# Half-norm statistics two and two behind the masks of the next two steps, and the second transposition of x1 behind the first half's feed-forward products

## The chip, the cores and the metric

The kernel runs on one core of one Trainium2 chip. The metric is the device time of one execution in microseconds. The matrix engine is called PE (its weight loads PEld), the vector engine DVE, the scalar engine ACT, GpSimd POOL, and SP issues most of the DMAs. Each engine works through its own instruction queue in order, and waits on semaphores for the others.

## What is computed

Sixteen graphs (`x`: 16 x 1024 x 128, one adjacency matrix 1024 x 1024 for all) go through three transformer-like layers and a last graph-attention layer. In short, for each batch element and layer:

```python
Q, K, V = h @ Wq, h @ Wk, h @ Wv                  # 8 heads of 16
scores = einsum('bnhd,bmhd->bhnm', Q, K) / sqrt(16)
scores = where(adj == 0, -inf, scores)
attn_out = einsum('bhnm,bmhd->bnhd', softmax(scores), V)
x = layer_norm(h + attn_out @ Wo + bo)            # norm 1, with gain and bias
y = relu(x @ W1 + b1) @ W2 + b2                   # 128 -> 256 -> 128
x = layer_norm(x + y)                             # norm 2
```

The last layer computes `h = x @ W`, an attention weight exp(leaky_relu(s_i + s_j)) over the neighbours, the weighted sum, adds x and normalises again. Everything is in float32.

## The kernel before, in words

**Blocks and steps.** The work is cut into 48 blocks, one for each batch element and layer (four batch elements go through the three layers in turn, so that blocks 0-3 are layer 0 of elements 0-3, blocks 4-7 layer 1, and so on). A block has 32 steps: 2 head groups x 2 halves of the queries x 8 key tiles (`kt`). A step (`score_step`) computes the scores of four heads as two PSUM tiles of 128 x 1024, by four matmuls (L423, "s"). Of these two tiles the second always gets its mask added by DVE (L433) and its exponential from ACT (L445); the first goes the same way where kt is 1, 5 or 7, and else gets its exponential first (ACT L430) and is multiplied by a 0/1 mask on POOL (L431). So a step has one or two DVE masks. There are three such PSUM slots ("s"), so the scores of a step have to wait until the masks or exponentials of the step before last and of the last one have read theirs. Four steps later (`AHEAD`) the exponentials are multiplied with V into one PSUM bank ("acc", L450). When a half of the queries has had its eight steps, `finish` reads this one bank with a DVE transposition (L461, "tt"), and the next accumulation has to wait for that.

In this document a step of a block is called step 0 to 31; M9 stands for the DVE mask of step 9 (M9a and M9b where there are two), E9 for the exponential after it, X10 for the exponential read straight from PSUM, P10 for the POOL mask.

**The other work is cut into pieces,** functions that are taken one a step by `piece()` behind the step's scores and products: the projections of the next block (`proj_tasks`: two transpositions, Wk, Wq and V by halves; `split` copies a half of K or Q out of PSUM as a rounded part "hi" by ACT, L385, and then the rest "lo" by DVE, L386), what follows the attention (`post_tasks`), and the last layer's pieces (`last_tasks`: nodes, edges, aggregates) for every batch element that has left its third layer. `post_tasks` has, for each half h of the nodes: `out_proj(h)` (32 small PE products with Wo), `x1t(h)` (four PE transpositions and an ACT copy; the second one also issues the two POOL operations of `scale_shift`), `ffn1(0, h)` and `ffn1(1, h)` (8 products and an ACT relu each) and `ffn2(h)` (64 small products). All of these go through one PSUM bank ("t"), so that a piece waits until the result of the piece before has been read.

**The steps at which pieces become due** are written in the table AT (L34). Before, the pieces behind the attention stood at steps 12 (out_proj 0), 22 (out_proj 1), 23 and 25 (x1t 0 and 1), 26, 27, 28 and 30 (ffn1), and 32 and 40 (ffn2, that is steps 0 and 8 of the block after). The projections are due at steps 3, 6, 9, 11, 14, 17, 19 and 20. The last layer's pieces have gaps instead of steps. A piece that is due has to wait where another chain's piece is taken in the same step.

**A half norm.** `out_proj` and `ffn2` end with `add_and_stats`: DVE adds the product to x (L329, with a raised priority), then come four `bn_stats` (L322) and four `bn_aggr` (L324), one for each of the half's four node tiles; then `normalise` issues seven operations on POOL (L337 to L341).

**Who sets the order.** PE and ACT run in the order in which the program issues (`manual_schedule`). DVE and POOL are ordered by the framework's scheduler by priorities, and their order is then fixed in the program too. `tc.issue_after(x)` makes instructions stand behind x; `behind["dve"]` is the last mask that DVE was given.

The two quoted lines are those that matter most below, the order of the pieces and the rule for a half norm:

```python
together = [(5, both, "+w +w"), (1, out_proj(0), "-w"), (1, out_proj(1), "-w"), (5, x1t(0), "+w"), (1, x1t(1), "+w")]
project([s["aT", h]], [w["Wo"]], h, add_and_stats(s["n1"]))
```

Of the kernel before, what the change touches and what calls it, by code (L numbers as in the profile page):

```python
# [30 lines left out]
FIRST = 1  # L31


AT = {"proj": (3, 6, 9, 11, 14, 17, 19, 20), "post": (12, 22, 23, 25, 26, 27, 28, 30, 32, 40, 41)}  # L34
AT_END = {3: (12, 21, 22, 24, 25, 26, 27, 28, 30, 31), 2: (8, 9, 13, 14, 15, 16, 17, 18, 20, 21)}
AHEAD = 4
BOTH_ON_DVE = (1, 5, 7)
# [78 lines left out]
def fast_path(ctx: ExitStack, tc: tile.TileContext, a: dict, out: bass.AP, flag):  # L116
    nc = tc.nc
# [201 lines left out]
    def stats(n, ts):  # L319
        z, st, mv = n  # L320
        for t in range(ts.start, ts.stop):
            nc.vector.bn_stats(st[:, t, :], z[:, t, :])  # L322
        for t in range(ts.start, ts.stop):
            nc.vector.bn_aggr(mv[:, t, :], st[:, t, :])  # L324

    def add_and_stats(n):
        def out(ts, ps):
            with soon():
                nc.vector.tensor_add(n[0][:, ts, :], v3(ps), n[0][:, ts, :])  # L329
            stats(n, ts)  # L330
        return out

    def normalise(n, ts):

# [64 lines left out]
    behind = {}  # L399
# [66 lines left out]
        return run  # L466


    def post_tasks(b, l):
        w = W[l]  # L470
        s = {}
        att, recs = state["A"], state["recs"]

        def gather(h):
            def run():
                s["aT", h] = half_tile("aT")
                nc.vector.transpose(s["aT", h], att[:, h].rearrange("p k g d -> p (k g d)"))
                if h == 1:
                    check_range(recs.rearrange("p g h k -> p (g h k)"))
            return run  # L480

        def out_proj(h):
            def run():
                if h == 0:
                    s["n1"] = with_stats(state["x", b])
                project([s["aT", h]], [w["Wo"]], h, add_and_stats(s["n1"]))
                normalise(s["n1"], slice(4 * h, 4 * h + 4))
            return run

        def x1t(h, alone=False):  # L490
            def run():
                x1 = s["n1"][0]
                s["x1T", h] = transpose_half("x1T", x1, h, w["ln1_gc"], w["ln1_bc"])
                if alone:
                    scale_shift(x1[:, 4 * h:4 * h + 4, :], w["ln1_g"], w["b2"])
                elif h == 1:
                    scale_shift(x1, w["ln1_g"], w["b2"])
            return run

        def ffn1(f, h):  # L500
            def run():
                s["h", f, h] = half_tile("hT")
                ps = bank()
                by_columns(ps, w["W1"][:, f * P:(f + 1) * P], s["x1T", h])
                with soon():
                    nc.scalar.activation(s["h", f, h], ps, AF.Relu, bias=w["b1"][:, f:f + 1], scale=1.0)
            return run

        def ffn2(h):
            def run():  # L510
                if h == 0:
                    s["n2"] = with_stats(state["x", b])
                project([s["h", f, h] for f in range(NF)], [w["W2"][:, f, :] for f in range(NF)], h,
                        add_and_stats(s["n2"]))
                normalise(s["n2"], slice(4 * h, 4 * h + 4))
            return run

        def both():
            gather(0)()
            gather(1)()  # L520


        together = [(5, both, "+w +w"), (1, out_proj(0), "-w"), (1, out_proj(1), "-w"), (5, x1t(0), "+w"), (1, x1t(1), "+w")]
        for h in range(2):
            together += [(1, ffn1(0, h), "+w"), (1, ffn1(1, h), "+w -w")]
        together += [(1, ffn2(0), "-w -w"), (1, ffn2(1), "-w -w")]
# [129 lines left out]
    chains = []  # L656
# [15 lines left out]
    def take(chain):  # L672

        _, f, tiles, mark, _ = chain["queue"][0]
        if any(free[t[1:]] == 0 for t in tiles.split() if t[0] == "+"):
            return False
        chain["queue"].popleft()
        f()
        for t in tiles.split():
            free[t[1:]] += -1 if t[0] == "+" else 1  # L680
        done.add(mark)
        chain["due"] = now[0]
        if not chain["queue"]:
            chains.remove(chain)
        return True

    def is_due(chain):
        gap, at = chain["queue"][0][0], chain["queue"][0][4]
        return now[0] >= (chain["due"] + gap if at is None else at)

    def piece():
        for chain in chains:
            if is_due(chain) and take(chain):
                return

    def need(mark):
        while mark not in done:
# [29 lines left out]
    def av_due(n):  # L727

        for item in [w for w in waiting if w[2] <= n]:
            step, e, _ = item  # L730
            half = step[:3]
            if half not in accs:
                if accs:
                    continue
                accs[half] = sums
                left[half] = NT
            waiting.remove(item)
            left[half] -= 1
            av_step(step, e, accs[half], left[half] == NT - 1, left[half] == 0)
            if left[half]:  # L740
                continue
            m, g, qh = half
            b, l = blocks[m]
            while g == 0 and qh == 0 and last_attn:
                need(last_attn.pop())
            finish(g, qh, accs.pop(half))()
            if m == len(blocks) - 1:
                if g == G - 1:
                    if qh == 0:
                        final.append(post_tasks(b, l)[1])  # L750
                    put(final[0][qh], ("final", qh), first=True)
                    if qh == 1:
                        put(last_tasks(b), ("last", b), chains[0])
            elif g == G - 1 and qh == 1:
                post = post_tasks(b, l)[0]
                chain = put(post[:1], ("attn", b, l))
                put(post[1:], ("post", b, l), chain, table=AT_END.get(len(blocks) - m))
                last_attn.append(("attn", b, l))
                if l == L - 1:
                    put(last_tasks(b), ("last", b), chain)  # L760
# [291 lines left out]
```

## Time and profile before

| what | value |
|---|---|
| median of 3 runs | 3961.19 us (3955.6 to 3964.78) |
| time of the profiled execution | 3958.22 us, span 3956.1 us, mean granted clock 0.988 |
| busy in the span | PE 95%, DVE 86%, ACT 85%, POOL 84% |
| masks on DVE (L433) | 2112, mean 1214 ns |
| `bn_stats` (L322), `bn_aggr` (L324) | 896 each, mean 278 and 154 ns |
| x add (L329), "tt" (L461), "lo" (L386) | mean 691, 706 and 680 ns |
| one block without last-layer pieces | 72.5 us |

The page gives for each engine its busy time, and by groups of instructions how long one takes and what ended the idle time before it. A view by windows gives the same for stretches of the span, with the clock that PE was granted (1.00 is full). The span falls into regular parts: blocks 2-9, 15-21, 27-33 and 39-45 take 72.5 us each; in blocks 11-14, 23-26 and 35-38 the last layer's pieces of four batch elements run as well, and they take 92.5 to 100.8 us; blocks 10, 22 and 34, where those begin, take 76.6 us. The rest is the start, blocks 46 and 47, and the end behind the last step.

### The profile page before, as it was taken

Reading aid. Unit: us, or ns where it says so; the run is one execution under the profiler, and the core shown is the slowest. Engines: PE = TensorE matmul, PEld = TensorE weight load, DVE = VectorE, ACT = ScalarE, POOL = GpSimd, SP = SyncE. Lnnn points to the kernel's source line nnn. Section 1 sums busy time; section 2 is a strip of 40 time slices with the busy share of each in tenths; the row PEclk is TensorE's granted clock in tenths of the full one; section 3 lists DMA queues with packets and bytes.
Section 4 is the critical chain, followed back from the end, with each engine's and each line's share of the span. In section 5 each row is a group of like instructions: output and inputs, shape, how many; then the busy total and the mean of one; then the engine's idle time right before and its main releaser. Section 6 shows DMA issues by size and latency. Waiting matters only on the chain.

```text
span 3956.1 us, 107747 instructions
## 1 busy us (share of the span) xinstructions
PE 3770.4 (95%) x44501; PEld 1552.3 (39%) x44501; DVE 3407.3 (86%) x5326; ACT 3371.7 (85%) x3961; POOL 3329.4 (84%) x3010
## 2 busy tenths in 40 slices
PE   7999999999999999999999999999999999999996
PEld 2333333344443333334444333333444433333345
DVE  7898998988888998988888898998888898898874
ACT  7999999977779999997777999999777799999860
POOL 5788988978789888988778898889877898898875
PEclk8999999999999999999999999999999999999998
DMA  6222222112222222222222222221222222222200
GB/s 164 65 65 57 53 65 65 49 43 65 55 58 61 65 65 54 55 65 56 55 56 56 65 54 56 65 65 47 56 55 56 68 50 59 65 56 54 66 8 20
DMA packets 124465, 233.13 MB, mean 59 GB/s; under 512 B 34624, under 2 KB 73792, under 8 KB 123968
## 3 DMA queue, kind: packets, MB, share of 16 engines
q1 hardware_dynamic: 123056, 225.74, 22.7%
q8 instruction: 354, 5.80, 0.6%
q14 instruction: 143, 1.17, 0.1%
q10 hardware_dynamic: 912, 0.42, 0.0%
HBM read 15.54 MB, written 8.39 MB: 6 GB/s over the span
## 4 chain that ended last, share of the span: by engine, by line
PE 66%; DVE 26%; POOL 3%; issue 3%; ACT 1%; SPq 0%; DMA 0%; DVEq 0%; POOLq 0%; ACTq 0%
PE acc L450 24%; PE t L297 20%; PE s L423 18%; DVE e L433 16%; DVE st L322 3%; PE t L286 2%; DVE tt L461 1%; DVE lo L386 1%; DVE mv L324 1%; POOL e L431 1%; PE s L297 1%; PE s L607 1%; DVE x L329 1%; POOL x L345 1%; DVE e L610 1%
## 5 line engine op out<-in xcount | busy, mean ns | idle before, releaser
L433 DVE TENSOR_TENSOR e<-s,mask_add 128x1024 f32<-128x1024 f32 x2112 | 2492.7, 1214 | 323.7 <-PE s L423 309.3
L445 ACT ACTIVATE e<-e 128x1024 f32<-128x1024 f32 x2112 | 2189.6, 1062 | 281.5 <-DVE e L433 266.7
L431 POOL TENSOR_TENSOR e<-e,mask 128x1024 f32<-128x1024 f32 x960 | 1934.3, 2028 | 300.5 <-ACT e L430 300.1
L450 PE MATMUL acc<-e,v 128*17 128x512 f32 x12288 | 1625.9, 601 | 32.1 <-DVE tt L461 23.0
L423 PE MATMUL s<-Wq,Wk 64*128 64x512 f32 x6144 | 1198.1, 458 | 62.1 <-DVE e L433 29.2
L430 ACT ACTIVATE e<-s 128x1024 f32<-128x1024 f32 x960 | 982.4, 1023 | 168.9 <-PE s L423 168.8
L423 PEld LDWEIGHTS s<-Wq,Wk 64*128 64x128 f32 x6144 | 500.1, 185 | 1046.0 <-issue 439.1
L450 PEld LDWEIGHTS acc<-e,v 128*17 128x17 f32 x12288 | 207.4, 95 | 538.1 <-issue 466.2
L341 POOL TENSOR_SCALAR x<-x,mv 128x128 f32<-128x128 f32 x896 | 389.7, 449 | 23.5
L337 POOL TENSOR_SCALAR mv<-mv 128x4 f32<-128x4 f32 x224 | 53.0, 237 | 236.2 <-DVE mv L324 188.6
L339 POOL TENSOR_TENSOR mv<-mv,half_neg 128x4 f32<-128x4 f32 x224 | 232.4, 1038 | 18.6
L345 POOL TENSOR_TENSOR x<-x,ln_g 128x1024 f32<-128x1024 f32 (+1 forms) x97 | 230.1, 2372 | 9.5 <-PE t L286 7.1
L297 PE MATMUL t<-hd,e 128*32 128x129 f32 x7040 | 208.3, 275 | 0.0
L329 DVE TENSOR_TENSOR x<-t,x 128x512 f32<-128x512 f32 x191 | 132.0, 691 | 83.5 <-PE t L297 77.1
L297 PEld LDWEIGHTS t<-hd,e 128*32 128x32 f32 x7040 | 194.7, 110 | 14.1 <-issue 4.7
L297 PE MATMUL t<-x1T,W 128*32 128x512 f32 x1520 | 198.2, 593 | 0.0
L322 DVE BATCH_NORM_STATS2 st<-x 128x6 f32<-128x128 f32 x896 | 196.4, 278 | 0.7
L297 PEld LDWEIGHTS t<-W,hT 128*32 128x32 f32 x6080 | 169.9, 110 | 58.5 <-issue 35.3
L297 PE MATMUL t<-W,hT 128*32 128x128 f32 x6080 | 183.4, 273 | 0.2 <-DVE x L625 0.2
L286 PEld LDWEIGHTS t<-identf,x 128*128 128x128 f32 x872 | 92.9, 141 | 230.3 <-issue 118.2
L286 PE MATMUL t<-identf,x 128*128 128x128 f32 x872 | 150.5, 288 | 33.5 <-DVE lo L386 19.6
L610 DVE SCALAR_TENSOR_TENSOR e<-s,mask 128x1024 f32<-128x1024 f32 x128 | 150.3, 1213 | 6.4 <-PE s L607 5.0
(118 smaller groups left out, 2569.5 us busy)
## 6 DMA issues: line engine op xcount, KB each, us to landing
Wk<-hi SPq DMA_DIRECT2D x384, 128.0 KB
Wk<-lo SPq DMA_DIRECT2D x384, 128.0 KB
Wq<-hi SPq DMA_DIRECT2D x384, 128.0 KB
Wq<-lo SPq DMA_DIRECT2D x384, 128.0 KB
x<-in_x_dram SPq DMA_DIRECT2D x16, 512.0 KB
out_dram<-x SPq DMA_DIRECT2D x31, 256.0 KB
ai<-in_adj_dram SPq DMA_DIRECT2D x8, 512.0 KB
g_rows<-parts SPq DMA_DIRECT2D x124, 4.0 KB
```

What stands on the lines that cost most here:

```text
L286: nc.tensor.transpose(ps[:, t * P:(t + 1) * P], src[:, 4 * h + t, :], identf)
L297: nc.tensor.matmul(dst[j:j + SLOT, :], lhsT[:, j:j + SLOT], rhs, start=start, stop=stop)
L322: nc.vector.bn_stats(st[:, t, :], z[:, t, :])
L339: nc.gpsimd.tensor_tensor(v, v, half_neg[:, ts], OP.pow)
L341: nc.gpsimd.tensor_scalar(z[:, t, :], z[:, t, :], mv[:, t, 0:1], mv[:, t, 1:2], op0=OP.add, op1=OP.mult)
L345: nc.gpsimd.tensor_mul(z, z, rows(gain, n))
L423: nc.tensor.matmul(ps[:, r * 512:(r + 1) * 512], k[64 * r:64 * r + 64, kt * P:(kt + 1) * P], q[64 * r:64 * r + 64, q0:q0 + 512], start=Tru ...
L430: nc.scalar.activation(ev, psv, AF.Exp, scale=HD ** -0.5)
L431: behind["pool"] = nc.gpsimd.tensor_mul(ev, ev, m).ins
L433: behind["dve"] = nc.vector.tensor_add(ev, psv, m).ins
L445: nc.scalar.activation(ev, ev, AF.Exp, scale=HD ** -0.5)
L450: nc.tensor.matmul(acc[j * SLOT:j * SLOT + HD + 1, :], v_bufs[m % 2][:, kt, 2 * j + g, :], e[:, j, :], start=first, stop=last)
```

## The change

In all blocks but those whose follow-up work belongs to the end (there `quick` stays true, and all is as before):

- The four `bn_stats` and four `bn_aggr` of a half norm are no longer issued right behind the x add. They become two pieces of their own: `first` has two `bn_stats`, `rest` the other two, the four `bn_aggr` and then `normalise`. Each is to stand behind the last DVE mask that was issued by then. Such a piece has a star and does not use up its step: another piece may be taken in the same step.
- The second transposition of x1 (`x1t(1)`) moves from step 25 to step 28, and the first half's two feed-forward products from 26 and 27 to 25 and 26; those of the second half from 28 and 30 to 30 and 31.
- `x1t(0)` has a gap of 1 where it had 5; its step in the table stays 23.

```diff
-AT = {"proj": (3, 6, 9, 11, 14, 17, 19, 20), "post": (12, 22, 23, 25, 26, 27, 28, 30, 32, 40, 41)}
+AT = {"proj": (3, 6, 9, 11, 14, 17, 19, 20), "post": (12, 13, 14, 22, 23, 23, 24, 25, 26, 28, 30, 31, 32, 33, 34, 40, 41, 42)}
...
-    def add_and_stats(n):
+    def add_and_stats(n, now=True):
         def out(ts, ps):
             with soon():
                 nc.vector.tensor_add(n[0][:, ts, :], v3(ps), n[0][:, ts, :])
-            stats(n, ts)
+            if now:
+                stats(n, ts)
         return out
+
+    def norm_later(n, h):
+
+        def first():
+            z, st, _ = n()
+            with tc.issue_after(behind["dve"]):
+                for t in range(4 * h, 4 * h + 2):
+                    nc.vector.bn_stats(st[:, t, :], z[:, t, :])
+
+        def rest():
+            z, st, mv = n()
+            with tc.issue_after(behind["dve"]):
+                for t in range(4 * h + 2, 4 * h + 4):
+                    nc.vector.bn_stats(st[:, t, :], z[:, t, :])
+                for t in range(4 * h, 4 * h + 4):
+                    nc.vector.bn_aggr(mv[:, t, :], st[:, t, :])
+            normalise(n(), slice(4 * h, 4 * h + 4))
+        return [(1, first, "*"), (1, rest, "*")]
...
-                project([s["aT", h]], [w["Wo"]], h, add_and_stats(s["n1"]))
-                normalise(s["n1"], slice(4 * h, 4 * h + 4))
+                project([s["aT", h]], [w["Wo"]], h, add_and_stats(s["n1"], quick))
+                if quick:
+                    normalise(s["n1"], slice(4 * h, 4 * h + 4))
...
-                        add_and_stats(s["n2"]))
-                normalise(s["n2"], slice(4 * h, 4 * h + 4))
+                        add_and_stats(s["n2"], quick))
+                if quick:
+                    normalise(s["n2"], slice(4 * h, 4 * h + 4))
...
+            together += [(1, out_proj(0), "-w")] + norm_later(n1, 0) + [(1, out_proj(1), "-w")] + norm_later(n1, 1)[:1]
+            together += [(1, x1t(0), "+w")] + norm_later(n1, 1)[1:]
+            together += [(1, ffn1(0, 0), "+w"), (1, ffn1(1, 0), "+w -w"), (1, x1t(1), "+w")]
+            together += [(1, ffn1(0, 1), "+w"), (1, ffn1(1, 1), "+w -w")]
+            together += [(1, ffn2(0), "-w -w")] + norm_later(n2, 0) + [(1, ffn2(1), "-w -w")] + norm_later(n2, 1)
...
     def piece():
-        for chain in chains:
-            if is_due(chain) and take(chain):
-                return
+        for chain in list(chains):
+            while chain["queue"] and is_due(chain):
+                alone = "*" not in chain["queue"][0][2]
+                if not take(chain):
+                    break
+                if alone:
+                    return
...
-                post = post_tasks(b, l)[0]
+                post = post_tasks(b, l, len(blocks) - m in AT_END)[0]
```

The number of instructions on each engine is the same in both programs; their order is not. Of DVE's order the program as built shows this for a block without last-layer pieces (steps 0 to 16; `st`, `mv`: statistics; `chk`, `recs`: small):

```
before: M0 x M1a st*4 mv*4 M1b M2 M3 tt M4 .. M8 aT*2 x M9a st*4 mv*4 M9b lo M10 M11 tt recs lo M12 x M13a st*4 mv*4 M13b M14 M15a lo M15b M16
after:  M0 x M1a M1b st*2 M2 st*2 mv*4 M3 tt M4 .. M8 aT*2 x M9a M9b lo M10 st*4 mv*4 M11 tt lo recs M12 x M13a M13b st*2 M14 M15a lo M15b st*2 mv*4 M16
```

More of the change, by code (lines that the diff above doesn't have):

```diff
@@ L466, in finish, with post_tasks @@
         return run
-    def post_tasks(b, l):
+    def post_tasks(b, l, quick=True):
         w = W[l]
@@ L520, in both, with n1, n2 @@
             gather(1)()
[L523 to L526, printed above, removed]
+        def n1():
+            return s["n1"]
+        def n2():
+            return s["n2"]
+        together = [(5, both, "+w +w")]
+        if quick:
+            together += [(1, out_proj(0), "-w"), (1, out_proj(1), "-w"), (5, x1t(0), "+w"), (1, x1t(1), "+w")]
+            for h in range(2):
+                together += [(1, ffn1(0, h), "+w"), (1, ffn1(1, h), "+w -w")]
+            together += [(1, ffn2(0), "-w -w"), (1, ffn2(1), "-w -w")]
+        else:
+            together += [(1, out_proj(0), "-w")] + norm_later(n1, 0) + [(1, out_proj(1), "-w")] + norm_later(n1, 1)[:1]
[3 more added lines that the diff above has]
+            together += [(1, ffn2(0), "-w -w")] + norm_later(n2, 0) + [(1, ffn2(1), "-w -w")] + norm_later(n2, 1)
         alone = [[(1, gather(h), "+w"), (1, out_proj(h), "-w"), (3, x1t(h, True), "+w"), (1, ffn1(0, h), "+w"),
@@ L678, in take @@
         f()
-        for t in tiles.split():
+        for t in tiles.replace("*", "").split():
             free[t[1:]] += -1 if t[0] == "+" else 1
```

## The prediction, made before the changed kernel was run

> **What bounds the kernel now.** I read the page first (busy shares), then the windows block by block, then the waits of one plain block, then its timeline. The page's first line shows four engines that are all busy:
>
> ```profile
> PE 3770.4 (95%) x44501; PEld 1552.3 (39%) x44501; DVE 3407.3 (86%) x5326; ACT 3371.7 (85%) x3961; POOL 3329.4 (84%) x3010
> ```
>
> The windows (start:end, length, then busy time of PE, PEld, DVE, ACT, POOL; clock; DMA) show one plain block (5) and blocks 11 to 14:
>
> ```profile
> 389.20:461.70 72.50, 71.11 (x726) 25.80 (x722) 65.19 (x97) 68.85 (x79) 64.59 (x57) 1.00 0.24 59
> ...
> 828.20:924.20 96.00, 91.51 (x1333) 44.30 (x1329) 82.30 (x141) 71.85 (x91) 76.46 (x75) 0.98 0.23 57
> 924.20:1021.30 97.10, 90.30 (x1334) 44.16 (x1331) 81.11 (x140) 72.10 (x91) 77.16 (x75) 1.00 0.22 56
> 1021.30:1122.10 100.80, 93.85 (x1341) 44.97 (x1337) 81.30 (x140) 73.04 (x92) 78.63 (x76) 0.97 0.21 55
> 1122.10:1214.70 92.60, 89.84 (x1286) 42.32 (x1282) 78.69 (x134) 69.92 (x81) 76.58 (x76) 1.00 0.23 59
> ```
>
> In a plain block PE is idle for 1.4 us of 72.5, ACT for 3.6, DVE for 7.3. The waits in that block (engine, line, releaser: total, times, longest) say how little of this is the matter of half norms:
>
> ```profile
> DVE e L433 <- PE s L423: 6.2, 10, 1.2
> ...
> ACT e L445 <- DVE e L433: 3.3, 5, 1.1
> ...
> PE s L423 <- ACT e L430: 0.5, 1, 0.5
> PE s L423 <- DVE e L433: 0.5, 2, 0.2
> PE acc L450 <- DVE tt L461: 0.4, 2, 0.2
> ```
>
> So DVE's idle time lies where PE has long pieces and DVE waits for scores; elsewhere DVE runs without a break. The DVE timeline (start, duration) of steps 9 to 12, then ACT's "hi" and PE's next accumulation:
>
> ```profile
> 410.02 0.69 DVE L329 TENSOR_TENSOR x<-t,x 128x512 f32<-128x512 f32 x1
> 410.63 1.21 DVE L433 TENSOR_TENSOR e<-s,mask_add 128x1024 f32<-128x1024 f32 x1
> 411.76 0.86 DVE L322 BATCH_NORM_STATS2 st<-x 128x6 f32<-128x128 f32 x4
> 412.54 0.36 DVE L324 BATCH_NORM_AGGREGATE mv<-st 128x2 f32<-128x6 f32 x4
> 412.82 1.19 DVE L433 TENSOR_TENSOR e<-s,mask_add 128x1024 f32<-128x1024 f32 x1
> 413.93 0.68 DVE L386 TENSOR_TENSOR lo<-t,hi 128x512 fp32r<-128x512 f32 x1
> 414.53 2.35 DVE L433 TENSOR_TENSOR e<-s,mask_add 128x1024 f32<-128x1024 f32 x2
> 416.79 0.70 DVE L461 STREAM_TRANSPOSE tt<-acc 128x512 f32<-128x512 f32 x1
> ```
> ```profile
> 412.90 0.57 ACT L385 CAST hi<-t 128x512 fp32r<-128x512 f32 x1
> ```
> ```profile
> 417.64 1.05 PE L450 MATMUL acc<-e,v 128*17 128x512 f32 x8 [0.18 <-DVE tt L461]
> ```
>
> To see: a mask takes 1.13 us of DVE (start to start), a half norm's eight statistics 1.06 (411.76 to 412.82), "lo" 0.60. "tt" comes after all of it, and PE's accumulation starts 0.85 behind "tt" (416.79 to 417.64). From step 1 to 19 it is DVE's sum of work, not the place of the statistics in it, that sets PE.
>
> **The change, in a plain block (29 of them).** Counts stay; 16 `bn_stats` and 16 `bn_aggr` a block (four bursts of 1.06 us) move. I laid the new order of DVE, ACT and PE on the rows of this block, with these intervals, and looked where PE leaves the old times. No DMA moves; SP's order is as before.
>
> *Steps 1 to 8 (norm 2, first half).* x add at 392.75 as before, since PE's ffn2 sets it. M1b comes 1.06 earlier, but the statistics still stand before "tt" of step 3, which starts at about 398.95 (before: 398.91). PE gains 0.24 in step 3 and loses it in front of the accumulation of step 4. ACT is 0.2 to 0.3 earlier, a slot of step 7 with it: -0.17. Bounds: 0 and -0.73 (what step 2 took above its 1.64).
>
> *Steps 9 to 12 (norm 2, second half).* Here the change adds a wait. "lo" stood behind M9b, and the statistics filled the time until "hi" was done (412.90 + 0.57 = 413.47). Now M9b starts at 411.67 and DVE is through with its issue at 412.80 (times 0.16 earlier by the step above); "hi" can't move, because on ACT it stands behind E9a, and E9a behind M9a. It ends at 413.32, so DVE stands for 0.56 in front of "lo". Behind it are M10, the four statistics, M11 and "tt", which starts at 417.28 in place of 416.79; PE's only accumulation bank waits for it: +0.49 at step 13, measured against before. Bounds: 0 if "hi" were ready, 0.6.
>
> *Steps 13 to 19 (norm 1, first half).* The second two statistics and the aggregates come behind M15b (the projection at 14 takes that step), in front of M16 and M17a. M17a is 0.78 late, of which 0.49 are inherited. E17a waits for it, "hi" of step 17 and X18 stand behind E17a on ACT, and the second slot of step 19 waits for X18: PE +0.72 at step 20, so this step adds 0.23. Bounds: 0 and 0.5.
>
> *Steps 23 to 25 (norm 1, second half).* The burst leaves M23b, which held step 25's first slot. But its second slot is set by x add, M23a, E23a, the copy of x1T and X24 in a row, which nothing moves: 0.
>
> *Steps 25 to 31.* x1t(1) at step 25 waited for its norm (the step took 2.74, and 2.23 without a wait as in step 6). At 28 it doesn't. The four ffn1 pieces take 2.50 wherever they stand. Steps 23 to 31 come to 0.27 less. One ffn1 relu falls behind E31, where ACT idles for 1.14 in step 2 anyway; the two POOL operations of `scale_shift` (2.4 each) go from behind P24 to behind P28, and ffn2's x add needs them only after step 32, some 3 us later: no cost; were POOL later by more than that, this add and M1a behind it would wait.
>
> Sum: 0.72 - 0.27 = +0.45 a block, 29 blocks: **+13 us**; bounds -0.1 and +0.8 a block.
>
> **Blocks 10 to 14 and their like (three groups).** Here pieces slip to other steps.
> - Block 11: the first edges come at step 1. DVE had the burst between M1a and M1b, then two edges, and PE stood:
>
> ```profile
> 835.81 0.50 PE L423 MATMUL s<-Wq,Wk 64*128 64x512 f32 x2 [1.66 <-DVE e L433]
> ```
> ```profile
> 836.00:840.00 4.00, 3.37 (x20) 0.97 (x22) 3.26 (x4) 2.53 (x3) 3.89 (x6) 0.77 0.73 169
> 840.00:844.00 4.00, 4.00 (x28) 1.11 (x22) 3.36 (x5) 3.21 (x5) 3.05 (x4) 0.81 0.02 6
> ```
>
>  After that wait the clock is 0.77 and 0.81 (0.23 x 4 + 0.19 x 4 = 1.7 us lost). Now the burst stands behind the edges and M2; the wait falls to about 0.6, and step 4 starts up to 2.6 earlier; taken as -1.9, since the clock may dip all the same. Waits for "lo" in steps 15 and 16 go (-1.1), others come in steps 25 to 31 (+0.6): -2.4.
> - Blocks 12 to 14: the first edges move from step 4 to 7, in front of a long piece (-1.0, -2.3, -1.5 for the three), and pieces leave crowded steps (15, 23 to 25, 29: together -3.7 in 12 and 13). Against it: "lo" of step 9 now stands behind M10 and an edge, and the aggregate of step 10 needs its bank: +1.3 in each. And the last aggregate slips from 16 to 21, so that POOL has between P22 and P24 a norm (3.5), `scale_shift` (4.9) and the end's pair (2.7): 11 us. P24 ends 16.6 us behind the start of step 22, the accumulation that needs it could start at 13.3: +3.3 in 12 and 13, and, by the row above, another clock dip (+1.7); x1t(1) follows `rest` by two steps there (+0.75; +0.5 in 14). In all about +2.4, +1.1 and 0.
> - Block 10: 0. A clock dip that only the first group has in block 13 (0.97 against 1.00) may go: -2.
>
> Group: -2.4 + 2.4 + 1.1 = +1, three of them +3, less 2: **+1 us**; bounds -15 and +25, as both waits on POOL and clock come or not. What else moves is named and costs nothing while POOL has its 8 us of idle time a plain block.
>
> [...]
>
> **Total:** +14. The profiled execution took 3958.2 (span 3956.1 and 2.1 around it), 0.07% under the median 3961.19; the share is the same, so 3961 + 14 = **3975 us**.
>
> **Rivals.**
> 1. *Faster, about 3932.* PE's gaps behind masks and exponentials (0.5 + 0.5 a block) were what the bursts cost; they vanish, 29 x 1.0. For it: the first x add's burst is followed by a gap of 0.52. Against it: "tt" behind the same sum of DVE work. It decides if "hi" of step 9 ends before M9b's issue does, that is 0.56 us earlier than its row lets it. 20%, with weaker forms down to 8 us 26%.
> 2. *No change, 3961.* DVE's sum sets the time of steps 1 to 19 and PE's the rest; the wait for "lo" is made good in the idle 0.5 and 1.0 us of DVE in steps 20 and 21. Against it: PE's queue is in order and doesn't win back a late accumulation. 18%.
> 3. *Slower, 4006.* POOL's 11 us starve block 14's kind too and each wait brings a clock dip (nine waits of 5 = 45 us in place of six: +15), plain blocks stand at their upper bound (+10), and block 11 keeps its dip (3 x 1.9 = +6): 3975 + 31. For it: blocks 12 and 13 already wait 0.7 twice for POOL at steps 23 and 24. Against it: in block 14 `scale_shift` is not in that queue. 8%.
>
> **How the numbers follow.** The forecast's case (3967 to 3995) has 48%, rival 3 8%: slower by more than 0.2% (8 us, about what this measurement can tell from no change) 0.56; same 0.18; faster 0.26. The range leaves out the strong form of rival 1 and the top of rival 3: 3940 to 4002.
>
> **What would show it.** Right: plain blocks of 72.8 to 73.0; an idle 0.5 us of DVE in front of "lo" released by ACT hi in step 10, PE's accumulation of step 12 waiting 0.9 for "tt"; step 25 without a wait for x; in blocks 12 and 13 a wait of PE for POOL's mask of 2 to 3 us at step 28, and a clock below 1.00 behind it; block 11 near 93. Wrong: plain blocks of 72.0 or less, or blocks 12 and 13 under 96.

## The result, and the profile after

The changed kernel takes 4022.6 us (median of 4 runs, 4020.03 to 4025.59); the kernel before, run beside it, 3962.53 (3955.6 to 3964.78). The ratio is 1.0155, with a 95% interval of 1.0137 to 1.0172. So it is slower by about 60 us. The forecast was 3975 us with a range of 3940 to 4002: the direction was right, and the loss was four times the one forecast. The profiled execution took 4020.03 us with a span of 4018.1, against 3956.1 before: 62 us to account for. Three executions were far longer than all others of their kernel (6930 us in run 3, 5043 in run 11, 4526 of the kernel before); the ratios leave them out, and no median moves by more than 1.1 us without them.

The page's busy shares of the changed kernel:

```profile
PE 3789.9 (94%) x44501; PEld 1563.3 (39%) x44501; DVE 3393.8 (84%) x5326; ACT 3363.7 (84%) x3961; POOL 3331.6 (83%) x3010
```

Instruction counts are the same and DVE, ACT and POOL are busy for about as long as before (3407.3, 3371.7 and 3329.4). PE's busy time is up by 19.5 us with the same number of matmuls, which fits its lower clock (0.984 against 0.988 over the span); the rest of the 62 us is waiting. The windows of the changed kernel (length; busy time of PE, PEld, DVE, ACT, POOL; clock; DMA) for one plain block (5) and the blocks 11, 12 and 14:

```profile
392.00:465.37 73.37, 70.93 (x725) 25.87 (x722) 64.84 (x97) 68.61 (x79) 64.61 (x57) 1.00 0.24 59
836.36:931.07 94.71, 91.05 (x1321) 43.77 (x1318) 81.03 (x140) 70.72 (x89) 76.11 (x74) 0.98 0.23 57
931.07:1035.18 104.11, 95.83 (x1333) 47.55 (x1329) 80.65 (x134) 72.10 (x91) 77.39 (x70) 0.95 0.21 53
...
1137.70:1234.99 97.29, 92.77 (x1296) 43.87 (x1292) 80.12 (x141) 71.29 (x82) 75.84 (x80) 0.98 0.22 57
```

A plain block went from 72.5 to 73.4, block 11 from 96.0 to 94.7, block 12 from 97.1 to 104.1, and block 14 from 92.6 to 97.3. With the starts of the scores as block borders, the sum is: 26 plain blocks x 0.90 = 23.4; the three plain blocks that follow a group (15 and its like, 74.0) 3 x 1.5 = 4.5; the three groups (blocks 10 to 14, means of three) 3 x 11.8 = 35.3; all else -1.

**A plain block.** The waits of block 5 (engine, line, releaser: total, times, longest):

```profile
PE acc L469 <- DVE tt L480: 1.5, 3, 0.8
...
DVE lo L405 <- ACT hi L404: 0.5, 1, 0.5
```

The first was 0.4 us in 2 before, the second is new. The DVE timeline of steps 9 to 12, the answer to the one in the prediction, then ACT's "hi" and PE's accumulation:

```profile
413.37 2.34 DVE L452 TENSOR_TENSOR e<-s,mask_add 128x1024 f32<-128x1024 f32 x2
416.24 0.69 DVE L405 TENSOR_TENSOR lo<-t,hi 128x512 fp32r<-128x512 f32 x1 [0.53 <-ACT hi L404]
416.85 1.22 DVE L452 TENSOR_TENSOR e<-s,mask_add 128x1024 f32<-128x1024 f32 x1
417.98 0.47 DVE L340 BATCH_NORM_STATS2 st<-x 128x6 f32<-128x128 f32 x2
...
419.04 1.19 DVE L452 TENSOR_TENSOR e<-s,mask_add 128x1024 f32<-128x1024 f32 x1
420.15 0.70 DVE L480 STREAM_TRANSPOSE tt<-acc 128x512 f32<-128x512 f32 x1
```
```profile
415.64 0.57 ACT L404 CAST hi<-t 128x512 fp32r<-128x512 f32 x1
```
```profile
421.00 1.05 PE L469 MATMUL acc<-e,v 128*17 128x512 f32 x8 [0.81 <-DVE tt L480]
```

M9a and M9b stand together, then DVE has nothing that may run for 0.53 us until "hi" is done; the statistics come later, in one burst behind M10, and "tt" and PE's only accumulation bank pay for it. Steps 9 to 12 take 0.63 us more. (They are one burst, not two and two: at step 9 the projection's piece is taken and ends the turn, so that both statistics pieces come at step 10.)

The second place is step 28, PE's timeline and then DVE's "tt":

```profile
455.94 0.85 PE L442 MATMUL s<-Wq,Wk 64*128 64x512 f32 x4
457.13 1.05 PE L469 MATMUL acc<-e,v 128*17 128x512 f32 x8 [0.34 <-DVE tt L480]
```
```profile
456.28 0.70 DVE L480 STREAM_TRANSPOSE tt<-acc 128x512 f32<-128x512 f32 x1
```

A half of the queries ends in step 27, and the accumulation of step 28 needs "tt". Before, a feed-forward product stood in step 27 and kept PE busy meanwhile. Now step 27 has no piece.

**The groups.** PE's waits in block 12 of the changed kernel:

```profile
PE acc L469 <- POOL e L450: 2.5, 1, 2.5
PE t L297 <- DVE lo L405: 1.5, 1, 1.5
...
PE s L642 <- DVE e L452: 1.1, 3, 0.6
PE s L442 <- DVE e L645: 0.6, 1, 0.6
```

The first is the wait for POOL's mask at step 28; the second is the aggregate at step 10, which needs the bank that "lo" reads; the last two belong to the edges, which now stand at steps 7, 10, 13 and 16 (4, 7, 10 and 13 before). Behind such waits the granted clock drops to 0.5 for 3.4 us: 16 such stretches in the groups, where the kernel before had the time of 5. Over the three groups, 35 us longer in sum, PE loses 18.8 us more to them (half of the time at half clock: 27.3 us against 8.5) and is idle for 9.7 us more; the rest is spread over its busy time. In the block 12 shown, 7.0 us longer, it has three such stretches and is idle for only 1.5 us more (8.3 against 6.8). One profile is not the whole measure of this: in run 4 below, whose groups stand as before, such stretches have the time of 12.

### The profile page after: what moved, and what is told of

Read it like the earlier page. It is cut to its first block, busy times and chain, and to the rows that moved or that the text cites. A ratio compares the mean times of both kernels' runs of the same rounds, so it can differ in the third digit from the quotient of the medians.

```text
span 4018.1 us, 107886 instructions
## 1 busy us (share of the span) xinstructions
PE 3789.9 (94%) x44501; PEld 1563.3 (39%) x44501; DVE 3393.8 (84%) x5326; ACT 3363.7 (84%) x3961; POOL 3331.6 (83%) x3010
## 4 chain that ended last, share of the span: by engine, by line
PE 55%; DVE 22%; POOL 12%; issue 5%; ACT 4%; DMA 0%; SPq 0%; DVEq 0%; POOLq 0%; ACTq 0%
PE acc L469 20%; PE t L297 17%; PE s L442 14%; DVE e L452 14%; POOL e L450 5%; POOL x L360 2%; PE t L286 2%; ACT e L449 2%; DVE lo L405 2%; DVE tt L480 1%; POOL x L364 1%; POOL x L365 1%; POOL mv L358 1%; ACT e L464 1%; DVE st L346 1%
## 5 line engine op out<-in xcount | busy, mean ns | idle before, releaser
L329 DVE TENSOR_TENSOR x<-t,x 128x512 f32<-128x512 f32 x191 | 130.1, 681 | 95.4 <-PE t L297 88.4
L286 PEld LDWEIGHTS t<-identf,x 128*128 128x128 f32 x872 | 92.1, 140 | 208.0 <-issue 116.8
L286 PE MATMUL t<-identf,x 128*128 128x128 f32 x872 | 145.3, 287 | 17.7 <-DVE lo L405 11.8
L405 DVE TENSOR_TENSOR lo<-t,hi 128x512 fp32r<-128x512 f32 x188 | 126.7, 674 | 23.5 <-ACT hi L404 23.5
L480 DVE STREAM_TRANSPOSE tt<-acc 128x512 f32<-128x512 f32 x192 | 135.5, 706 | 4.6 <-PE acc L469 4.4
```

The lines of the kernel that those rows point to most:

```text
L286: nc.tensor.transpose(ps[:, t * P:(t + 1) * P], src[:, 4 * h + t, :], identf)
L405: nc.vector.tensor_sub(lo[:, c], ps, hi[:, c].bitcast(F32))
```

## The experiments

Step times below are taken from the starts of the scores; block values of groups are means over the three groups. A table with all runs stands at the end of this section.

**1. The order alone:** the changed kernel with all four half norms at once (`ffn2` like `out_proj`, and no `norm_later` in the list).

```diff
-AT = {"proj": (3, 6, 9, 11, 14, 17, 19, 20), "post": (12, 13, 14, 22, 23, 23, 24, 25, 26, 28, 30, 31, 32, 33, 34, 40, 41, 42)}
+AT = {"proj": (3, 6, 9, 11, 14, 17, 19, 20), "post": (12, 22, 23, 25, 26, 28, 30, 31, 32, 40)}
...
-                project([s["aT", h]], [w["Wo"]], h, add_and_stats(s["n1"], quick))
-                if quick:
+                project([s["aT", h]], [w["Wo"]], h, add_and_stats(s["n1"]))
+                if True:
```

> Only the order and the steps of x1t(1) and the feed-forward products are those of the changed kernel; the statistics stand behind the x add as before. Theory A (two waits make the plain blocks slower: 'lo' for 'hi' at step 10, from the late statistics, and the accumulation of step 28 for 'tt', from the missing piece at step 27; the groups lose by late pieces and halved clock): no wait of DVE for 'hi' at step 10, step 12 at 2.8 as before; step 25 loses its 0.5 of waiting for x, step 28 is 2.7 to 2.8 in place of a ffn1 step without a wait; a plain block 72.4 to 72.6 (before 72.48, changed 73.4), the whole 3955 to 3975. Theory B (DVE's sum of work sets the pace, and a wait that is taken away at one place comes back at the next, so that single steps tell nothing): about half of the changed kernel's loss, 3990, with the loss in steps 2 to 20 as well.

Measured: 3971.36 us, ratio 1.0031 (1.0019 to 1.0044); a plain block 72.85. No wait for "hi", step 12 at 2.78; step 28 at 2.76. Step 25 takes 2.78 with a feed-forward product in it (2.50 without a wait), so x1t(1)'s 0.51 of waiting is not all won: steps 25 to 31 take 16.36 us against 16.06. The order costs 0.30 of the 0.90 us, and step 2 0.13 more (2.50 against 2.37). The whole fits theory A, the plain block is 0.25 above it.

**2. A long piece at step 27 again.**

```diff
-AT = {"proj": (3, 6, 9, 11, 14, 17, 19, 20), "post": (12, 13, 14, 22, 23, 23, 24, 25, 26, 28, 30, 31, 32, 33, 34, 40, 41, 42)}
+AT = {"proj": (3, 6, 9, 11, 14, 17, 19, 20), "post": (12, 13, 14, 22, 23, 23, 24, 25, 27, 28, 30, 31, 32, 33, 34, 40, 41, 42)}
```

> The changed kernel with the first half's second feed-forward product at step 27 in place of 26, so that step 27 has its long piece again, and step 26 none. Theory A: the accumulation of step 28 no longer waits for 'tt' (0.34 in the changed kernel); step 27 back at 2.5, step 26 at 1.65, step 28 at 2.2 to 2.3 in place of 2.76; a plain block 0.5 shorter (72.9), 29 of them -15 us, the whole about 4007, give or take 6 for the groups. Theory B: step 28 gets shorter but steps 29 to 31 or 0 take it back: the whole 4018 to 4026.

Measured: 4012.96 us, 1.0137 (1.0120 to 1.0154); a plain block 73.13. Step 28 is back at 2.23, but step 27 takes 2.70 and not 2.50, and step 31 0.07 more. The wait at step 28 is gone: the waits of block 5 in this run have only the other two for "tt".

```profile
PE acc L469 <- DVE tt L480: 1.2, 2, 0.8
```

So theory A's mechanism holds and its price was too high: step 28 wins 0.53, of which 0.34 is the wait, but with the empty step now at 26, steps 27 and 31 take 0.27 more, and 0.27 a block is won.

**3. Norm 2's second half at once.**

```diff
-                        add_and_stats(s["n2"], quick))
-                if quick:
+                        add_and_stats(s["n2"], quick or h == 1))
+                if quick or h == 1:
...
-            together += [(1, ffn2(0), "-w -w")] + norm_later(n2, 0) + [(1, ffn2(1), "-w -w")] + norm_later(n2, 1)
+            together += [(1, ffn2(0), "-w -w")] + norm_later(n2, 0) + [(1, ffn2(1), "-w -w")]
```

> The changed kernel, but the second half of norm 2 (ffn2 at step 8) has its statistics right behind the x add, as before. Theory A: DVE doesn't stand in front of 'lo' at step 10, step 12 comes back from 3.4 to 2.8; a plain block 72.8 or, if M17a is then no longer late, 72.5 (changed 73.4): -18 to -26 us in the plain blocks. In blocks 12 to 14 of a group 'lo' of step 9 is early again, so the 1.4 us gap of PE at step 10 and the half clock behind it go: 2 to 3 us in each of nine blocks, -18 to -27. Whole: 3970 to 3987. Theory B: 'tt' of step 11 stands behind the same sum of DVE's work, the time moves by less than 8 us. If the half clock isn't the gap's consequence but comes from the load over the block: as many half-clock stretches as in the changed kernel (16 in the groups).

Measured: 3994.03 us, 1.0081 (1.0061 to 1.0102), 7 us above theory A's range; a plain block 72.76. Step 12 is 2.77 again, as theory A says: this is 0.62 of the 0.90 us. In the groups only part came, and of the 16 half-clock windows 11 are left. Steps 0 to 26 of blocks 12 and 13 are those of the kernel before or nearly so, the edges stand at 4, 7, 10 and 13 again, and block 14 takes 92.2; but blocks 12 and 13 stay at 102, with the loss now in steps 27 to 29:

```profile
1017.51 1.62 PE L286 MATMUL t<-identf,x 128*128 128x128 f32 x4 [2.28 <-POOL x L360]
```

x1t(0) waits for norm 1's first half, whose product with Wo was done at step 12. Its statistics came at steps 25 and 26 (DVE L340 and L346 at 1011.3 to 1012.8): a statistics piece is looked at only when no earlier chain takes a piece in the step, and in these blocks there is one in nearly every step from 13 to 24. In the changed kernel itself that wait is absent: with the other pieces two steps later, step 15 of blocks 12 and 13 was free of them, the same statistics came at step 16 and x1t(0) found its norm done. Block 12 of the changed kernel:

```profile
987.58 0.47 DVE L340 BATCH_NORM_STATS2 st<-x 128x6 f32<-128x128 f32 x2
```

So the late turn becomes a cost when the slip is undone. And the edges moved because the last layer's first piece is due 5 steps behind the piece before it in its chain, which is ffn2(1) here and was the second statistics piece in the changed kernel.

**4. The groups as before.**

```diff
...
-                post = post_tasks(b, l, len(blocks) - m in AT_END)[0]
+                old = len(blocks) - m in AT_END or m >= 9 and m % 12 in (9, 10, 11, 0, 1)
+                post = post_tasks(b, l, old)[0]
...
```

With `old`, `quick` is true and the pieces stand at the steps of the kernel before (12, 22, 23, 25, 26, 27, 28, 30, 32, 40).

> The changed kernel, but in the blocks where the last layer's pieces run (the follow-up work of blocks 9 to 13, 21 to 25, 33 to 37) both the statistics and the order are those of before. Theory A: blocks 11 to 14 and their like come back to 96, 97, 100, 93, and the half-clock stretches in the groups from 16 to about 4; the plain blocks stay at 73.4: the whole 4022 - 36 = 3982 to 3992. Theory B (the clock of the whole run is lower, or the plain blocks lose more when the groups are undisturbed): less than half of that comes back, above 4003.

Measured: 3988.23 us, 1.0071 (1.0054 to 1.0087): the groups are 34 us of the loss and the plain blocks (73.41) the rest, as theory A has it. Blocks 12 and 13 are at 97.2 and 99.3. The half clock did not do as expected: its profile has 12 windows of it in the groups, not about 4.

**5. The last layer's first piece two steps earlier.**

```diff
-        return [(5, xt(0), "+w +last +w +w"), (1, xt(1), "+w"), (2, nodes(0, 3), ""), (2, nodes(3, 6), ""), (2, nodes(6, 8), "-w -w"),
+        return [(3, xt(0), "+w +last +w +w"), (1, xt(1), "+w"), (2, nodes(0, 3), ""), (2, nodes(3, 6), ""), (2, nodes(6, 8), "-w -w"),
```

> The changed kernel, but the last layer's first piece is due 3 steps behind the piece before it in place of 5. In the changed kernel that piece is the second statistics piece (step 10), before it was ffn2(1) (step 8), so that edges and aggregates slip; with 3 the edges of blocks 12 to 14 stand at steps 4, 7, 10 and 13 again. Theory A (three causes in the groups: the slip; 'lo' of step 9 late behind the next mask; statistics pieces that get no turn while other pieces are taken, so that x1t(0) of blocks 12 and 13 waits for its norm at step 27): the slip's part goes, the other two stay. Block 14: 92.2 as without the late second half, plus 1.4 of PE standing at step 10 and 0 to 1.7 of half clock = 93.6 to 95.3 (changed 97.3); blocks 12 and 13: 102 plus the same = 103 to 105 (changed 101.9), with a wait of about 2.3 in front of x1t(0) at step 27; block 15 and its like 73.4 (74.0). Whole 4012 to 4028. Theory B (the slip alone makes the groups slow, a late 'lo' costs nothing there): block 14 at 92.2, blocks 12 and 13 at 102, whole about 4005.

Measured: 4023.48 us, 1.0156 (1.0140 to 1.0171), within theory A's range and the same as the changed kernel, in sum: block 14 falls from 97.3 to 93.0 and block 15 from 74.0 to 73.4, blocks 12 and 13 rise to 102.7 and 103.3 with the 2.3 us in front of x1t(0), and block 11 by 1.1.

```profile
1139.32:1232.31 92.99, 89.95 (x1281) 42.44 (x1280) 79.70 (x135) 70.55 (x81) 77.18 (x75) 1.00 0.24 60
```

Block 14 lies between the two theories. Step 10 takes 6.12 there, as before: with the edges at their old steps DVE's order has "lo" right behind M9b, though the statistics are still late. So the 1.5 us at step 10 belong to the slip and not to the late statistics, against theory A; 0.77 stay at step 13.

**6. Statistics pieces first.**

```diff
     def piece():
+        for chain in list(chains):
+            while chain["queue"] and is_due(chain) and "*" in chain["queue"][0][2]:
+                take(chain)
```

together with run 3's edit.

> As the run with the second half of norm 2 at once, and besides that the statistics pieces that are due are taken ahead of any other piece of the step, whatever chain that is in. Theory A: in blocks 12 and 13 the statistics of norm 1's first half come at steps 13 and 14 and not at 25 and 26; x1t(0) at step 27 no longer waits for the norm (2.3 us in the run without this), step 27 comes from 5.6 to 2.2, 28 and 29 from 3.2 and 3.3 to 2.2 to 3.0, and the halved clock behind that wait goes: blocks 12 and 13 at 97 to 99 in place of 102; plain blocks 72.76; whole 3994 - 6 x 5 = 3964 (3958 to 3972). Theory B (POOL's load in these steps, a norm, scale_shift and the end's pair in a row, makes the wait, not the late turn): x1t(0) or a POOL mask still keeps PE for 1.5 to 2.5 there; whole 3984 to 3996.

Measured: 3976.81 us, 1.0036 (1.0023 to 1.0049). Blocks 12 and 13 are at 97.7 and 98.3 and step 27 at 2.24: theory A. But block 11 rose from 96.3 to 99.5, which neither had: with statistics on time PE waits 2.4 us at its step 20 for POOL's mask, behind which the clock halves in two of the three groups, and the whole lies between the two ranges. POOL works without a break from 887.2 to 901.4 us (two norms, the end's pair, the first half of a `scale_shift`) until that mask is done: POOL's load, theory B's cause, decides in that block. The kernel before has norm 1's statistics there at step 13, this run at steps 13 and 15, which points to norm 1's split; no run has that split alone.

**7. Only x1t(1) and one feed-forward product exchanged, in the kernel before.**

```diff
-        together = [(5, both, "+w +w"), (1, out_proj(0), "-w"), (1, out_proj(1), "-w"), (5, x1t(0), "+w"), (1, x1t(1), "+w")]
-        for h in range(2):
-            together += [(1, ffn1(0, h), "+w"), (1, ffn1(1, h), "+w -w")]
+        together = [(5, both, "+w +w"), (1, out_proj(0), "-w"), (1, out_proj(1), "-w"), (5, x1t(0), "+w")]
+        together += [(1, ffn1(0, 0), "+w"), (1, x1t(1), "+w"), (1, ffn1(1, 0), "+w -w")]
+        together += [(1, ffn1(0, 1), "+w"), (1, ffn1(1, 1), "+w -w")]
```

> The kernel before, with one thing changed: the second transposition of x1 and the first half's first feed-forward product change places (x1t(1) from step 25 to 26, ffn1(0, 0) from 26 to 25); statistics as before, step 27 keeps its long piece. Theory A (x1t(1)'s wait for its norm at step 25, 0.5 us, is the only thing that the change's new order could win, and the missing piece at step 27 gave it back): step 25 at 2.78, step 26 at 2.23, steps 27 and 28 at 2.50; a plain block 72.49 - 0.23 = 72.26, whole 3961 - 7 = 3954 (3950 to 3958). Theory B (the time comes back in the steps behind it, or x1t(1) waits at 26 instead): 3958 to 3965.

Measured: 3963.83 us, 1.0005 (0.9996 to 1.0014). Step 25 is 2.78 and step 26 2.23, as theory A says; a plain block 72.32, since step 2 takes 0.07 more. Those 26 x 0.17 = 4.4 us don't show in the whole, which falls in theory B's range. In the profiled execution the groups give them back (+1.9 us each, with 10 windows of half clock against 5); whether this is so in the other runs can't be seen from their times.

**8. Changed kernel with 5 and the new lines of 6 together.**

```diff
-        return [(5, xt(0), "+w +last +w +w"), (1, xt(1), "+w"), (2, nodes(0, 3), ""), (2, nodes(3, 6), ""), (2, nodes(6, 8), "-w -w"),
+        return [(3, xt(0), "+w +last +w +w"), (1, xt(1), "+w"), (2, nodes(0, 3), ""), (2, nodes(3, 6), ""), (2, nodes(6, 8), "-w -w"),
...
     def piece():
+        for chain in list(chains):
+            while chain["queue"] and is_due(chain) and "*" in chain["queue"][0][2]:
+                take(chain)
```

> The changed kernel with both: the last layer's first piece due after 3 steps, and statistics pieces that are due taken ahead of others. What stays is 'lo' late behind the next mask at steps 9 and 10, and the plain blocks' two waits. Theory A: plain blocks 73.4; blocks 12 and 13 at 97 to 98.6 plus 1.4 to 3 for 'lo' = 99 to 101, block 14 93.6 to 95.3, block 15 73.4: 4022 - 3 x (1.9 + 1.9 + 2.8 + 0.6) = 4000 (3990 to 4008). Theory B (the statistics cost as much wherever they are put in the crowded steps 9 to 14): 4012 or more.

Measured: 3981.42 us, 1.0051 (1.0035 to 1.0066), 9 us below theory A's range. Blocks 12 to 14 are at 97.2, 97.9 and 92.1, so slip and late turn were all of the loss there. A plain block is 73.0: `first` now gets its turn at step 9, so that its two `bn_stats` stand in front of "lo" and fill most of DVE's wait for "hi" (0.14 us of idle time left), and step 12 takes 3.01. The windows of block 12, then PE's wait in block 11:

```profile
935.77:1032.85 97.08, 90.50 (x1333) 44.04 (x1329) 80.99 (x140) 71.81 (x91) 77.97 (x75) 1.00 0.22 56
```
```profile
PE acc L469 <- POOL e L450: 2.4, 1, 2.4
```

**9 and 10. The split at steps 1 and 2, alone and with the exchange of 7.** Norm 1 and norm 2's second half at once, the first half of norm 2 split over steps 1 and 2; the order as before (9) or with the exchange (10).

```diff
-AT = {"proj": (3, 6, 9, 11, 14, 17, 19, 20), "post": (12, 13, 14, 22, 23, 23, 24, 25, 26, 28, 30, 31, 32, 33, 34, 40, 41, 42)}
+AT = {"proj": (3, 6, 9, 11, 14, 17, 19, 20), "post": (12, 22, 23, 25, 26, 27, 28, 30, 32, 33, 34, 40)}
...
+            together += [(1, out_proj(0), "-w"), (1, out_proj(1), "-w"), (1, x1t(0), "+w")]
+            together += [(1, ffn1(0, 0), "+w"), (1, x1t(1), "+w"), (1, ffn1(1, 0), "+w -w")]     # 10
             together += [(1, ffn1(0, 1), "+w"), (1, ffn1(1, 1), "+w -w")]
+            together += [(1, ffn2(0), "-w -w")] + norm_later(n2, 0) + [(1, ffn2(1), "-w -w")]
```

> The kernel before, but with the statistics of norm 2's first half alone (ffn2 at step 0) split over steps 1 and 2; norm 1 and the second half at once, the order of x1t(1) and the feed-forward products as before. Theory A (of the four splits the one at steps 1 and 2 is harmless or a gain, the loss lies in the others and in the order): plain blocks 72.43 (-0.06); in block 11 the wait of 1.66 at step 2 is 0.6 shorter, steps 1 and 4 to 7 of blocks 11, 13 and 14 come as in the run with the second half at once: -1 to -2.5, -0.5, -0.5; three groups -6 to -10; whole 3950 to 3957. Theory B (the time in the groups depends on where the halved clock falls, and a wait taken away there shows nowhere): 3957 to 3966.

> As the run with only norm 2's first half split, and x1t(1) and ffn1(0, 0) change places (steps 26 and 25) as in the run of the swap alone, which had plain blocks of 72.32. Theory A: the two gains add, since they lie in steps 1 to 7 and 25 to 26, and the 0.07 that step 2 lost in the swap (its mask behind the burst) goes: plain blocks 72.2 to 72.27; whole 5 to 8 below the run without the swap, 3943 to 3951. Theory B (POOL's scale_shift one step later makes step 2 or the groups wait): no gain over the run without the swap, 3952 to 3962.

Measured: 3953.46 us, 0.9981 (0.9972 to 0.9990), and 3948.25 us, 0.9969 (0.9957 to 0.9980). Both beat both kernels, within theory A's totals, but in part by luck, since its plain blocks were wrong: 72.61 and 72.53, because PE's accumulation now waits 0.48 and 0.56 for a POOL mask at step 18 (2.17 and 2.25 against 1.65), of which step 19 gives 0.27 back. The gain is in the groups: block 13 at 97.9 and 98.0 (99.4 before), 14 at 92.0 and 91.7 (92.6), 11 at 95.1 and 94.6 (96.0). The wait at step 18 of block 5 and the window of block 13, both of run 10:

```profile
431.74 1.05 PE L469 MATMUL acc<-e,v 128*17 128x512 f32 x8 [0.56 <-POOL e L450]
```
```profile
1021.76:1119.71 97.95, 91.48 (x1341) 44.27 (x1337) 81.20 (x140) 72.67 (x92) 78.70 (x76) 1.00 0.23 56
```

**11. Changed kernel with 2, 3 and 6 together.**

```diff
-AT = {"proj": (3, 6, 9, 11, 14, 17, 19, 20), "post": (12, 13, 14, 22, 23, 23, 24, 25, 26, 28, 30, 31, 32, 33, 34, 40, 41, 42)}
+AT = {"proj": (3, 6, 9, 11, 14, 17, 19, 20), "post": (12, 13, 14, 22, 23, 23, 24, 25, 27, 28, 30, 31, 32, 33, 34, 40, 41, 42)}
...
-                        add_and_stats(s["n2"], quick))
-                if quick:
+                        add_and_stats(s["n2"], quick or h == 1))
+                if quick or h == 1:
...
     def piece():
+        for chain in list(chains):
+            while chain["queue"] and is_due(chain) and "*" in chain["queue"][0][2]:
+                take(chain)
```

> The changed kernel with three edits together: norm 2's second half at once, statistics pieces that are due taken ahead of others, the first half's second feed-forward product at step 27. Theory A (these waits are the whole loss, except block 11's wait of 2.4 for POOL at step 20, which comes when its statistics are on time): plain blocks 72.75 - 0.27 = 72.48, blocks 12 to 14 at 97 to 98.6 and 93, block 11 at 98 to 100; whole 3977 - 8 = 3969 (3964 to 3974). Theory B (something else of the change costs too, in steps 13 to 19 or 23 to 25): plain blocks 72.6 or more, whole above 3975.

Measured: 3964.47 us, 1.0010 (1.0000 to 1.0020); a plain block 72.47, blocks 11 to 14 at 99.0, 97.1, 97.7 and 92.5, as theory A has it. With the named waits gone the plain blocks are back at the value before, though three of the four splits and the late x1t(1) are still in; block 11 keeps its wait for POOL.

| run | plain | 11 | 12 | 13 | 14 | ratio |
|---|---|---|---|---|---|---|
| before | 72.49 | 96.0 | 97.3 | 99.4 | 92.6 | 1 |
| changed | 73.40 | 94.7 | 101.9 | 101.9 | 97.3 | 1.0155 |
| 1 order alone | 72.85 | 95.4 | 97.3 | 98.6 | 93.6 | 1.0031 |
| 2 piece at 27 | 73.13 | 93.3 | 101.9 | 102.0 | 97.3 | 1.0137 |
| 3 second half at once | 72.76 | 96.3 | 101.6 | 102.7 | 92.2 | 1.0081 |
| 4 groups as before | 73.41 | 97.3 | 97.2 | 99.3 | 94.1 | 1.0071 |
| 5 gap of three | 73.40 | 95.8 | 102.7 | 103.3 | 93.0 | 1.0156 |
| 6 statistics first | 72.75 | 99.5 | 97.7 | 98.3 | 93.1 | 1.0036 |
| 7 exchange alone | 72.32 | 96.9 | 97.3 | 99.7 | 93.1 | 1.0005 |
| 8 both of 5 and 6 | 73.00 | 98.8 | 97.2 | 97.9 | 92.1 | 1.0051 |
| 9 first half only | 72.61 | 95.1 | 97.1 | 97.9 | 92.0 | 0.9981 |
| 10 and exchange | 72.53 | 94.6 | 97.2 | 98.0 | 91.7 | 0.9969 |
| 11 all three undone | 72.47 | 99.0 | 97.1 | 97.7 | 92.5 | 1.0010 |

## Why the prediction was right or wrong

| step of the prediction | forecast, us a block | measured |
|---|---|---|
| steps 0 to 8 | -0.17 | -0.05 |
| steps 9 to 19 | +0.89 | +0.66 |
| steps 20 to 31 | -0.27 | +0.30 |
| plain block | +0.45 | +0.91 |
| block 11 | -2.4 | -1.2 |
| block 12 | +2.4 | +4.7 |
| block 13 | +1.1 | +2.5 |
| block 14 | 0 | +4.8 |
| block 10 | 0 | +1.0 |

- *Steps 9 to 12, the wait for "lo": right.* Forecast 0.56 us of DVE idle (its own times, 412.80 and 413.32, give 0.52) in front of "lo" behind ACT's "hi", "tt" late, PE's accumulation 0.85 behind it; measured 0.53 and a gap of 0.81. Run 3 takes it away and wins 0.64 a block. Steps 13 to 19 were to add 0.23 and added 0.03.
- *"Steps 25 to 31 ... come to 0.27 less": the step that failed in the plain blocks.* Its half on x1t(1) was right: with step 27 kept filled, the exchange of run 7 wins 0.23 in steps 25 and 26. What failed is "the four ffn1 pieces take 2.50 wherever they stand". That holds for the piece itself where it doesn't wait, but its place was cover: in step 27 it hid DVE's "tt" from the accumulation of step 28. The forecast asked what hides each moved piece and not what each moved piece had been hiding. Runs 1 and 2 show the wait (0.34, with 0.27 a block won back by a piece at 27); from steps 20 to 31 the miss is 0.57 a block, 16 us over 29 blocks, and 0.53 of it is step 28 (2.76; 2.23 without a wait).
- *The groups, "+1 us": the step that failed most, 34 us.* What moves was read right (edges from step 4 to 7, the last aggregate from 16 to 21, P24 behind 11 us of POOL work), and the waits it named came: 2.5 at step 28 against a forecast of 3.3, 1.5 at step 10 against 1.3. The gains set against them (-1.0, -2.3, -1.5 and -3.7 for pieces out of crowded steps) mostly did not last, since the pieces make other steps crowded: the edge now shares step 7 with no aggregate, but its masks stand in front of the scores of step 8 (two gaps of 0.63, not forecast), and step 13 takes 6.89 against 6.12. The cause is the slip by two steps: run 5 undoes it, and the waits at steps 8, 10 and 28 are gone and block 14 is at 93.0. In blocks 12 and 13 statistics that get no turn then take its place; run 8 without both has the three blocks at 97.2, 97.9 and 92.1. For step 10 the forecast's own reason, an edge in front of "lo", held; late statistics, the reason in run 5's theory A, did not, since run 5 has them and no such wait. Block 10, put at 0, shows the plain blocks' 0.63 at step 12.
- *Half clock: the mis-sized term.* One dip of 1.7 us, as read behind block 11's wait in the profile before, was counted behind each of the six POOL waits, 10 us. Measured: five of those six waits have one, but there are 16 windows of half clock in the groups against 5, also behind the waits at steps 8 and 10. At up to 1.7 us each the 11 more are up to 19 us. How many of them are chance stays open: with the groups as before, run 4's profile had 12. The 1.66 us that the forecast read as enough for a dip stood with a second wait of 0.63 us at 836.94; the window in front of that dip had 1.7 us of idle time from both.
- *The rivals.* "Faster" needed "hi" to be ready 0.56 us earlier; it was not. "No change" needed idle DVE time in steps 20 and 21 to make up for the late accumulation; PE took 2.52 and 1.65 there as before. "Slower, 4006" was nearest: plain blocks at the upper bound of +0.8 (measured 0.91), more dips, and block 11's dip kept, in all three groups. Its POOL starvation in block 14's kind did not come; that block's loss was elsewhere.
- *Its signs.* The waits for "lo" (0.53) and "tt" (0.81) came, and in blocks 12 and 13 those for POOL (2.2 to 2.5 us) with a lower clock. The plain blocks (73.4, not 72.8 to 73.0) and block 11 (94.7, not near 93) are outside what it called right.

## What to carry to other kernels

When a piece is moved out of a step, ask what it was hiding there: here the accumulation of step 28, which needs its only bank, waited 0.34 us for "tt" once nothing long stood in front of it, and with that the step cost 0.53 us more, as much as the moved piece's own wait had (0.51). A queue that counts its due times from the piece before it moves as a whole when small pieces are added to its end; here two cheap pieces moved edges and aggregates by three to five steps, which cost block 14 4.3 us (97.3 against 93.0 in run 5). Splitting work "behind later masks" is not free even at the same instruction count: of four splits, one won when it was alone (run 9), one cost 0.63 us a plain block (run 3), and norm 1's two were not run alone.

## What the runs showed of the hardware that was not expected

The granted clock of PE stood at 0.5 in stretches that fit one grid in each of the two profiles. Between 500 and 3700 us of the span the kernel before has 4 of them and the changed kernel 16; 19 are 3.413 us long and one, of the kernel before, 6.827. Within each profile their starts lie whole multiples of 3.4133 us apart, to within 0.001 of that length. Cut at these multiples, that part of the two profiles has 1737 windows at full clock in which PE was busy for 80% or more, and none of them was followed by a halved one; of 105 between 50% and 80% 12 were, of 9 below 50% 8. Of the 21 halved windows one was followed by a second, with PE busy for 2.97 of its 3.41 us. Two windows of the changed kernel, the second with the clock at 0.50:

```profile
960.81:964.22 3.41, 1.87 (x17) 0.63 (x16) 3.10 (x4) 2.13 (x3) 2.01 (x1) 1.00 0.02 5
964.22:967.63 3.41, 3.41 (x64) 3.13 (x68) 1.07 (x1) 0.00 (x0) 0.00 (x0) 0.50 0.02 5
```

and two of the kernel before, where a gap of 1.47 us lies across their border, 1.33 of it in the first and 0.13 in the second, and no halved window followed:

```profile
984.90:988.31 3.41, 2.08 (x16) 0.50 (x12) 3.40 (x4) 2.78 (x4) 3.18 (x6) 1.00 0.00 0
988.31:991.72 3.41, 3.28 (x50) 1.97 (x52) 1.91 (x3) 3.23 (x5) 3.33 (x3) 1.00 0.06 17
```

So a wait of about 1.5 us cost its length in one place (1.47), and its length (1.54) and up to 1.7 us more, half of a halved window, in the other; that this goes by where the wait falls on the grid is an estimate from these rows and was not shown. Block 12 of the changed kernel took 104.1 in one group and 100.8 in another of the same execution (clock 0.95 and 0.98), and block 13 of the kernel before 100.8, 98.8 and 98.6 (0.97, 1.00 and 1.00). What separates windows of 50 to 80% that are followed by a halved one from those that are not stays open.
